# Feed-forward blocks: the first tile's attention scores in two groups of matmuls instead of one

## The chip, the cores and the metric

The kernel runs on one core of a Trainium2 chip. A core has five engines that work side by side: TensorE (matmuls, called PE in the profile, with PEld for the loading of its weights), VectorE (DVE), ScalarE (ACT), GpSimd (POOL) and SyncE (SP, which only issues transfers here). The metric is the device time of one execution in microseconds (us), lower is better.

A matmul on TensorE has a stationary operand, which is loaded into the array first (a weight load), and a moving operand, which streams past it. In the profile `64*128` ahead of a shape means that the stationary operand takes 64 rows and 128 columns of the array; `64x128` after it is the output or operand shape of one record. For 32-bit floats the profile shows each matmul of the program as two records of a matmul and two of a weight load.

## The reference, cut to what matters

The input is 16 sequences of 256 tokens with 128 features. Four blocks follow one another, each added to its input: a state-space block, a feed-forward block, a power-attention block, and the same feed-forward block again. The change touches the feed-forward blocks. Such a block has two layers, and each layer begins with local attention over 8 heads of 64 features, in windows of 64 tokens:

```python
bt = jnp.arange(n).reshape(w, WINDOW)            # WINDOW = 64, n = 256
sim = jnp.einsum('bhwid,bhwjd->bhwij', bq, bk)   # own window and the one before
mask = (i < j) | (i > j + WINDOW) | (j == -1)
sim = jnp.where(mask, -jnp.finfo(sim.dtype).max, sim)
attn = jax.nn.softmax(sim, axis=-1)
out = jnp.einsum('bhwij,bhwjd->bhwid', attn, bv)
```

A query sees the keys of its own window that are not later than itself, and those of the window before that are at most 64 tokens back. After the attention come a projection, a layer norm, a gated unit with 341 hidden features, and the residual sums.

## The kernel before, in words

**Tiles and stages.** In a feed-forward block (`ffn_block`, line 644) one item of work is one sequence in one layer, 32 items per block. An item's 256 tokens are two tiles of 128, called t = 0 and t = 1. Two items form a group, which later shares the gated unit. For each item and tile the stages of the attention are: project to queries, keys and values (`f_qk`, `f_pv`), rotate and normalise on VectorE and GpSimd (`f_m`), transpose on TensorE (`f_qkT_ps`, copied to `f_qkT`), lay the mask into a PSUM tile (`mask`, line 833, tile `f_sim`), add the scores to it (`scores`, line 840), take the row maximum (`maxima`, line 857, tile `f_mx`), subtract it, take the exponential and normalise (`f_pr`), transpose the weights (`f_ppt`, copied to `f_prT`), weigh the values (`weigh`, line 889, tile `f_po`) and project back (`f_pw`).

**The scores.** `f_sim` has 128 queries on the partitions and, along the free axis, two halves of heads (r), four head pairs (p) and 128 keys. Its two halves r lie in two PSUM banks. The mask copy puts 0 where a score counts and -1e30 where not; the matmuls accumulate on top of it. Head r of pair p lies in rows 64 r to 64 r + 63 of `f_qkT`, so that its matmul uses that half of the array's rows. For t = 0 all 128 queries meet all 128 keys in one matmul per head, eight in all: stationary 64 rows by 128 columns (the queries), moving 128 keys. For t = 1 each window of 64 queries meets the 128 keys of its window and the one before: sixteen matmuls, stationary 64 by 64, moving 128 keys. `weigh` is the reverse: for t = 0 eight matmuls with a stationary operand of 128 rows by 64 columns and 128 moving columns, for t = 1 sixteen with 128 by 64 and 64 moving columns.

**What sets the order.** Each engine runs its instructions in the order in which the program writes them: the class `Pinned` (line 69) ties every instruction to the one before it on its engine, and so line 89 is the line of nearly every record. Within the block the order is written by hand in the string `period` (line 1005): `s0.1:3` stands for `scores` of tile 0 of the second item of the group that was begun three periods earlier. One period holds two items' worth of every stage, so four calls of `scores`, two of them with t = 0. There are 16 periods of groups in a block, and a few more at the ends in which the pipeline fills and empties.

Of the kernel before, what the change touches and what calls it, by code (L numbers as in the profile page):

```python
# [20 lines left out]
P = 128  # L21
# [8 lines left out]
DH = 64  # L30
WINDOW = 64
# [15 lines left out]
def kernel(ctx: ExitStack, tc: tile.TileContext, io, out: bass.AP, blocks=BLOCKS):  # L47
# [515 lines left out]
    NP = HEADS // 2  # L563
# [80 lines left out]
    def ffn_block(k, fw, store):  # L644
# [14 lines left out]
        pe, dve, act, pool, sp = (Pinned(e) for e in (nc.tensor, nc.vector, nc.scalar, nc.gpsimd, nc.sync))  # L659
# [32 lines left out]
        psim = ps_sim.tile([P, 2, NP, P], F32, name=f"f{k}_sim_first", tag="sim")  # L692
# [146 lines left out]

        def scores(n, q, t):  # L840
            psim, qkT = q["sim", t], q["qkT"]
            for p in range(NP):
                for w in range(t + 1):
                    for r in range(2):
                        rows = slice(r * DH, (r + 1) * DH)
                        if t == 0:
                            out_, q0, nq, k0 = slice(0, P), 0, P, 0
                        else:
                            out_, q0, nq, k0 = (
                                slice(w * WINDOW, (w + 1) * WINDOW), P + w * WINDOW, WINDOW, (w + 1) * WINDOW  # L850
                            )
                        pe.matmul(
                            psim[out_, r, p, :], qkT[rows, 0, p, q0 : q0 + nq], qkT[rows, 1, p, k0 : k0 + P],
                            start=False, stop=True, skip_group_check=True,
                        )

        def maxima(n, q, t):
            mx = q["mx", t] = sb.tile([P, 2, NP], F32, name=f"f{k}_mx_{n}_{t}", tag="mx", bufs=4)
# [127 lines left out]
        def unit_sum(g, q):  # L986
# [10 lines left out]
            ns=norm_stats, nf=norm_factors, n=norm, ut=turn_tokens, uc=turned_tokens, p=project, sq=squares,  # L997
            ro=rotate, ss=square_sums, ra=rotated, v=values, vc=values_out, b=bounded, i=inverses,
            nw=newton, no=normed, t=turn, tc=turned, k=mask, s=scores, mx=maxima, lm=less_maximum,
            e=exponentials, su=sums, wo=weights_of, wt=turn_weights, wc=turned_weights, we=weigh,  # L1000
            oc=weighed, mi=mix, ma=mixed, Us=unit_stats, Uf=unit_factors, Un=unit_norm, Ut=unit_turn,
# [413 lines left out]
```

## Time and profile before

| | us |
|---|---|
| median of three runs | 2185.27 (2184.02 to 2185.98) |
| the profiled execution | 2186.17 |
| its span, from the first to the last instruction | 2184.2 |
| TensorE busy in the span | 2032.0 (93%) |
| GpSimd busy | 1900.1 (87%) |
| VectorE busy | 1839.4 (84%) |
| ScalarE busy | 1708.2 (78%) |

The first feed-forward block's score matmuls lie between 519 and 1115 us of the span, the second's between 1544 and 2140 us. The profile gives for each group of like instructions the shape, the count, the busy time, the mean of one and the idle time ahead of it. Its chain of waits follows back from the last instruction to what released each step; a stretch in which that chain holds one engine alone, piece after piece, is a stretch in which that engine sets the time.

### The profile page before, as it was taken

Reading aid. Unit: us, or ns where it says so; the run is one execution under the profiler, and the core shown is the slowest. Engines: PE = TensorE matmul, PEld = TensorE weight load, DVE = VectorE, ACT = ScalarE, POOL = GpSimd, SP = SyncE. Lnnn points to the kernel's source line nnn. Section 1 sums busy time; section 2 is a strip of 40 time slices with the busy share of each in tenths; the row PEclk is TensorE's granted clock in tenths of the full one; section 3 lists DMA queues with packets and bytes.
Section 4 is the critical chain, followed back from the end, with each engine's and each line's share of the span. In section 5 each row is a group of like instructions: output and inputs, shape, how many; then the busy total and the mean of one; then the engine's idle time right before and its main releaser. Section 6 shows DMA issues by size and latency. Waiting matters only on the chain.

```text
span 2184.2 us, 44223 instructions
## 1 busy us (share of the span) xinstructions
PE 2032.0 (93%) x16172; PEld 1333.4 (61%) x16174; DVE 1839.4 (84%) x3285; ACT 1708.2 (78%) x2879; POOL 1900.1 (87%) x2183
## 2 busy tenths in 40 slices
PE   5999999877999999999986999997899999999998
PEld 2344444334667777777773777775567777777775
DVE  1999999997988888888844999996999888888883
ACT  4777777746888887878854999997788887878874
POOL 6899999968999888888954999996999988888993
PEclk8999999998999999999996999999999999999999
DMA  4333333320100111101102332330010110001110
GB/s 91 97 83 81 98 80 78 80 49 20 24 23 16 23 23 23 23 16 23 23 11 82 118 118 86 112 118 2 21 24 22 23 23 17 23 22 33 28 28 23
DMA packets 97349, 104.21 MB, mean 48 GB/s; under 512 B 51458, under 2 KB 63596, under 8 KB 97132
## 3 DMA queue, kind: packets, MB, share of 16 engines
q1 hardware_dynamic: 96444, 101.22, 18.0%
q8 instruction: 129, 2.11, 0.4%
q14 instruction: 88, 0.72, 0.1%
q10 hardware_dynamic: 688, 0.15, 0.0%
HBM read 40.28 MB, written 2.36 MB: 20 GB/s over the span
## 4 chain that ended last, share of the span: by engine, by line
PE 58%; POOL 18%; DVE 11%; issue 8%; ACT 3%; DMA 1%; SPq 1%; POOLq 0%; DVEq 0%; ACTq 0%
PE f_qk L89 8%; POOL bx L89 7%; PE f_sim L89 5%; PE f_po L89 5%; PE f_pw L89 5%; PE f_qkT_ps L89 4%; PE f_ppt L89 4%; PE f_pv L89 4%; PE f1m_ag L89 3%; PE f3m_ag L89 3%; POOL f_m L89 3%; PE psc L89 3%; DVE z L89 2%; DVE hs L89 2%; DVE psc L89 2%
## 5 line engine op out<-in xcount | busy, mean ns | idle before, releaser
L89 POOL TENSOR_TENSOR f_m<-f_m 128x256 f32<-128x256 f32 x512 | 360.8, 729 | 30.9 <-DVE f_m L89 30.7
L89 DVE TENSOR_TENSOR f_m<-f_qk,rope 128x1024 f32<-128x1024 f32 x256 | 309.0, 1217 | 24.5 <-POOL f_m L89 16.4
L89 DVE TENSOR_TENSOR_SCAN hs<-a,bx 128x1024 f32<-128x1024 f32 x128 | 291.6, 2284 | 39.8 <-POOL bx L89 28.4
L89 POOL TENSOR_TENSOR bx<-dx,bb 128x1024 f32<-128x1024 f32 x128 | 298.7, 2361 | 4.6 <-DVE hs L89 3.9
L89 PE MATMUL f_qk<-wqkv,f_hT 128*128 128x512 f32 x512 | 261.8, 604 | 1.8 <-ACT f_hT L89 1.8
L89 POOL TENSOR_TENSOR f_m<-f_m,f_rn 128x512 f32<-128x512 f32 x256 | 263.3, 1045 | 0.2
L89 POOL TENSOR_TENSOR f_pr<-f_pr,f_rl 128x1024 f32<-128x1024 f32 x128 | 241.7, 1899 | 23.1 <-PE f_po L89 14.4
L89 PE MATMUL y_ps<-hs,ident 128*128 128x512 f32 x512 | 242.9, 599 | 11.5 <-DVE hs L89 6.6
L89 ACT ACTIVATE a<-delta,neg_a 128x510 f32<-128x510 f32 x256 | 176.1, 689 | 78.9 <-DVE hs L89 73.3
L89 ACT ACTIVATE f_sq<-f_qk 128x512 f32<-128x512 f32 x256 | 154.6, 605 | 60.5 <-PE f_qk L89 56.5
L89 ACT COPY f_qkT<-f_qkT_ps 128x512 f32<-128x512 f32 x256 | 147.3, 590 | 63.4 <-PE f_qkT_ps L89 62.7
L89 PEld LDWEIGHTS y_ps<-hs,ident 128*128 128x128 f32 x512 | 95.5, 190 | 154.6 <-issue 126.0
L89 POOL TENSOR_TENSOR z<-z,mx 128x1024 f32<-128x1024 f32 x96 | 180.8, 1896 | 7.9 <-DVE mx L89 5.6
L89 DVE TENSOR_REDUCE f_mx<-f_sim 128x8 f32<-128x1024 f32 x128 | 153.3, 1198 | 31.7 <-PE f_sim L89 31.7
L89 DVE TENSOR_REDUCE f_ss<-f_sq 128x8 f32<-128x512 f32 x256 | 173.0, 677 | 7.8 <-ACT f_sq L89 7.5
L89 PEld LDWEIGHTS f_qkT_ps<-ident,f_m 128*128 128x128 f32 x1024 | 121.2, 142 | 83.7 <-issue 50.9
L89 DVE TENSOR_TENSOR f_pr<-f_sim,f_mx 128x1024 f32<-128x1024 f32 x128 | 155.7, 1216 | 0.4
L89 PE MATMUL f_qkT_ps<-ident,f_m 128*128 128x128 f32 x1024 | 147.2, 277 | 9.4 <-POOL f_m L89 9.4
L89 DVE TENSOR_REDUCE f_rl<-f_pr 128x8 f32<-128x1024 f32 x128 | 152.9, 1194 | 1.9 <-ACT f_pr L89 1.9
L89 ACT COPY f_prT<-f_ppt 128x512 f32<-128x512 f32 x256 | 144.4, 595 | 6.5 <-PE f_ppt L89 5.8
L89 PE MATMUL f_sim<-f_qkT 64*64 64x128 f32 (+1 forms) x3072 | 145.6, 279 | 3.6 <-ACT f_sim L89 2.3
L89 PE MATMUL f_po<-f_prT,f_vx 128*64 128x64 f32 (+1 forms) x3072 | 144.4, 243 | 4.7 <-DVE f_m L89 2.4
(206 smaller groups left out, 5086.7 us busy)
## 6 DMA issues: line engine op xcount, KB each, us to landing
bb<-reps SPq DMA_DIRECT2D x128, 256.0 KB
pdk<-pngd SPq DMA_DIRECT2D x64, 512.0 KB
f_vx<-f_vx SPq DMA_DIRECT2D x128, 128.0 KB
f_shifted<-u_all SPq DMA_DIRECT2D x64, 64.0 KB
f_shifted<-u_all SPq DMA_DIRECT2D x64, 63.5 KB
x_all<-in_resid_dram SPq DMA_DIRECT2D x8, 256.0 KB
out_dram<-x_all SPq DMA_DIRECT2D x8, 256.0 KB
wqkv<-in_wqkv_dram SPq DMA_DIRECT2D x6, 256.0 KB
```

Source lines behind the costliest of these rows:

```text
L89: bi = getattr(self.eng, name)(*args, **kw)
```

## The change

Only `scores` changes, and only for t = 0. The eight matmuls become sixteen in two groups. The first group has all 128 queries as the stationary operand, as before, but only the first 64 keys as the moving one. The second group has the last 64 queries as the stationary operand (64 rows by 64 columns, output partitions 64 to 127) and the other 64 keys as the moving one. The quarter in which the first 64 queries meet the later 64 keys is wholly masked; it now keeps what the mask copy put there. For t = 1 the matmuls and their order are as before.

```diff
         def scores(n, q, t):
             psim, qkT = q["sim", t], q["qkT"]
-            for p in range(NP):
-                for w in range(t + 1):
-                    for r in range(2):
-                        rows = slice(r * DH, (r + 1) * DH)
-                        if t == 0:
-                            out_, q0, nq, k0 = slice(0, P), 0, P, 0
-                        else:
-                            out_, q0, nq, k0 = (
-                                slice(w * WINDOW, (w + 1) * WINDOW), P + w * WINDOW, WINDOW, (w + 1) * WINDOW
+            if t == 0:
+                pieces = [(slice(0, P), 0, 0, WINDOW, 0), (slice(WINDOW, P), WINDOW, WINDOW, WINDOW, WINDOW)]
+            else:
+                pieces = [
+                    (slice(w * WINDOW, (w + 1) * WINDOW), P + w * WINDOW, (w + 1) * WINDOW, P, 0) for w in range(2)
+                ]
+            for group in ([[c] for c in pieces] if t == 0 else [pieces]):
+                for p in range(NP):
+                    for out_, q0, k0, nk, at in group:
+                        for r in range(2):
+                            rows = slice(r * DH, (r + 1) * DH)
+                            nq = out_.stop - out_.start
+                            pe.matmul(
+                                psim[out_, r, p, at : at + nk], qkT[rows, 0, p, q0 : q0 + nq],
+                                qkT[rows, 1, p, k0 : k0 + nk], start=False, stop=True, skip_group_check=True,
                             )
-                        pe.matmul(
-                            psim[out_, r, p, :], qkT[rows, 0, p, q0 : q0 + nq], qkT[rows, 1, p, k0 : k0 + P],
-                            start=False, stop=True, skip_group_check=True,
-                        )
```

The order of everything else, on every engine, stays what it was, and so do the waits.

## The prediction

> **What bounds the kernel now.** I read the profile's summary page first, then a table of windows over the feed-forward blocks, then the chain of waits there, then the groups by shape. The summary says that TensorE is busy 93% of the span and holds 58% of the chain; both are averages. The windows show where it is full (columns: window in us; busy us and count for PE, PEld, DVE, ACT, POOL; granted clock, DMA share, GB/s):
>
> ```profile
> 640.00:700.00 60.00, 60.00 (x562) 42.81 (x559) 54.39 (x91) 52.48 (x93) 57.57 (x80) 1.00 0.09 21
> 700.00:800.00 100.00, 100.00 (x906) 71.66 (x905) 85.31 (x120) 81.06 (x141) 88.46 (x123) 1.00 0.09 21
> ...
> 1100.00:1180.00 80.00, 58.60 (x412) 40.42 (x410) 28.65 (x64) 36.66 (x60) 34.91 (x47) 0.81 0.15 40
> ```
>
> In the middle of a block TensorE is never idle, at full clock, while VectorE (85 of 100 us) and GpSimd (88) have slack. "Busy" alone is weak for matmuls, since they are pipelined and their ends are modelled. The chain of waits decides (start, length, what, count of records):
>
> ```profile
> 1073.28 0.86 PE f1m_ag L89 x2
> 1074.14 0.89 PE f_pw L89 x8
> 1075.03 1.09 PE f_sim L89 x16
> 1076.12 1.09 PE f_pw L89 x8
> ...
> 1082.40 0.87 PE f_ppt L89 x8
> 1083.27 1.02 PE f_po L89 x16
> 1084.29 1.03 PE f_sim L89 x32
> 1085.33 1.06 PE f_qk L89 x2
> 1086.38 0.86 PE f1m_ag L89 x2
> 1087.24 0.87 PE f_qkT_ps L89 x8
> 1088.12 1.08 PE f_po L89 x32
> 1089.20 1.09 PE f_pw L89 x8
> ```
>
> It is TensorE group after TensorE group, no wait on another engine between. That holds from 615.24 to about 1115 us in the first block and from 1640.51 to about 2140 us in the second; between 640 and 1110 us no matmul shape has any idle time before it (0.0 in each row). So TensorE time added there is added to the end one for one. Before 615.24 and 1640.51, while the pipeline fills, the chain runs through GpSimd and VectorE (`POOL f_m`, `DVE f_m`), and TensorE waits up to 1.2 us at a time.
>
> **Prices, from those lines.** `f_sim x16` is one call of the scores for t = 0: 16 records, 1.09 us. They run two at a time, one in each half of the array's rows, so 8 waves. `f_pw x8` takes 0.89 us after `f1m_ag` and 1.09 us after `f_sim`: 0.20 us for changing how the array is divided (draining it, then a first weight load of 128 columns with nothing to hide it). `f_qk x2` says the same: 0.86 against 1.06. So `f_sim x16` is 0.20 + 8 waves of 0.111.
>
> For a stationary operand of 64 columns the entry is cheaper by the shorter first load. By shape:
>
> ```profile
> L89 PEld LDWEIGHTS f_sim<-f_qkT 64*128 64x128 f32 x1024 | 62.7, 189 | 14.7 <-issue 4.5 <-ACT f_qkT L89 3.7 <-ACT f_sim L89 2.3
> L89 PEld LDWEIGHTS f_sim<-f_qkT 64*64 64x64 f32 x2048 | 55.2, 132 | 13.9 <-issue 7.8 <-ACT f_sim L89 2.3 <-ACT f_vx L89 1.5
> ```
>
> The mean load record is 189 ns with 128 columns, 132 ns with 64, the rows being the same 64. The difference, 0.057, is the half of a load that runs at some 0.11 us per 128 columns plus a fixed part. So entry is about 0.15 us for 64 columns (`f_qkT_ps x4` after `f_po`, 0.58 against 0.44 elsewhere, fits). From `f_po`: x16 is 8 waves with 64 stationary and 128 moving columns, (1.02 - 0.15) / 8 = 0.109 us; x32 is 16 waves with 64 and 64, (1.08 - 0.15) / 16 = 0.058 us. A wave therefore seems to last as long as the longer of its weight load and its stream, 0.11 us per 128 columns either way, the next load running under the present stream.
>
> **The change part by part.**
>
> *First group (A), 128 queries by 64 keys.* The stream falls from 0.107 to about 0.053 us a wave; the loads are the same 16 records of 128 columns. No row of the trace has a load longer than its stream, so I bound a wave: from below 0.058 us, the `f_po x32` wave (loads free); from above 0.165 us, load 0.11 and stream 0.055 one after the other. I take 0.111: the load alone already needs that, and in `f_sim` and `f_pw`, where both are 128 columns, the two together fit into 0.111, so they overlap. Only the last wave, with no load behind it, ends about 0.05 us sooner. A: 0.20 + 8 x 0.111 - 0.05 = 1.04 us.
>
> *Here a rule of the Trainium skill is weighed.* The page "TensorE: Matmul & The Clock Gate", section "Back-to-back issue gap", lets the gap between matmuls fall with the number of moving columns; by that alone A would be 0.20 + 8 x 0.058 = 0.66 us. Its section "LDWEIGHTS (loading the stationary operand)" says that a load takes columns / 1.2 ns whatever the rows: 107 ns for 128, 53 for 64, which is this trace's 57 ns of difference. This speaks against the change, since A halves the stream and leaves the load. The sum would be 0.38 us per call lower by the first rule; I go with the second, since the load rows carry it.
>
> *Second group (B), 64 queries by 64 keys.* All new: 8 matmuls, 16 matmul and 16 load records of 64 by 64, again two at a time. Price by `f_po x32`, which has 64-column loads and 64-column streams at the same rate of records: 8 x 0.058 = 0.46 us.
>
> *Between A and B.* The array goes from 64 x 128 to 64 x 64 divisions. The trace has no such step, but every step in which the columns change shows the price (`f_po` 128*64 to `f_pw` 128*128: 1.09 against 0.89). Bounds: nothing, B's first loads pulled under A, or 0.15 us. I take 0.15, as the change of columns alone is priced so elsewhere. "TensorEngine Tiling (Array Packing)", section "Key Properties", has it that a change of tiling mode, not of tile, drains the array; without the rule the sum would be 0.15 less. B: 0.61 us.
>
> *One call:* 1.04 + 0.61 - 1.09 = +0.56 us. After it the next group pays its entry of 0.20, as now.
>
> *Everything else.* The mask copy, the maximum and all later stages are the same instructions with the same waits; no DMA, no SP or POOL instruction moves. The maximum (`f_mx` on DVE) waits for B's last matmul and starts 0.56 us later relative to the group's start; behind it in VectorE's queue stand `f_ss` and `f_pr`, and ACT's exponential waits for those. Their slack (15 of 100 us on VectorE) takes that, since all of it moves with TensorE. The 1024 more matmul records and as many loads must be fetched; `f_po x32` already runs at B's rate of records with no idle time, so nothing is added.
>
> *How many count.* 64 calls: 1024 records of 64*128 / 16. In each block six start before 615.24 or 1640.51 and 26 after. 52 x 0.56 = 29.1 us on the path. Of the twelve early ones, one is on the chain, at a lower clock:
>
> ```profile
> 519.11 0.85 PE f_qkT_ps L89 x4
> 519.97 1.67 PE f_sim L89 x16
> 521.63 1.05 PE f_pv L89 x2
> ```
>
> It pays 0.56 x 1.67 / 1.09 = 0.86 us. The other eleven lie before TensorE waits for GpSimd or VectorE, which hide them; without that cover they would cost 6 us more. The sum is 29.1 + 0.9 = 30.0 us: span 2184.2 to 2214.2, the profiled execution's 2186.17 to 2216.2. The median of the runs shown is 0.9 us under that execution: **2215.3 us**, 1.4% slower. Anything within 0.2% (4.4 us) I count as the same, about what a measurement of this kernel can tell from no change.
>
> **Rivals.**
>
> 1. *Likeliest, 65%:* as above. Its own range is 2209 to 2222: a few hidden calls more or fewer, entry or wave off by a tenth, and the 6 us at the high end.
> 2. *No drain between A and B, 16%:* rows stay 64, and B's first loads go into the array under A's streams. For it: loads and streams overlap everywhere else. Against: each change of columns in the chain costs. 0.15 less per call: +0.41 x 52 + 0.6 = 22 us, 2207.
> 3. *The shorter stream pays, 10%:* A's waves at 0.058, by loads faster than their records say. 0.66 + 0.61 - 1.09 = +0.18, x 52 = 10 us with the early one, 2195. Against it the load rows.
> 4. *Load and stream don't overlap when the stream is short, 6%:* A's wave 0.165, +0.48 a call more, 1.04 x 52 = 54 plus 1, 2240. For it: no row shows a long load under a short stream.
> 5. *Not slower, 3%:* TensorE's fullness is an artefact of modelled ends, and another engine sets the period of about 39 us. Then the 1.13 us of two calls per period go into idle time, and it stays at 2185 to 2186. It decides once TensorE has 1.13 us of true slack per period (2.9%). For it: GpSimd at 88 of 100. Against: entries and groups have the same length each time and the chain has no other engine in it for 500 us.
>
> **How the numbers follow.** Cases 1 and 2 hold 81%; together they span 2202 to 2226 with 2207's and 2215's own errors, so that is the range; cases 3, 4 and 5 are out. Slower by over 0.2%: 1 to 4, 96% after 1% for a case 3 that shrinks into the noise; same 3%; faster 1%, for what I have not thought of.
>
> **What would show it.** In the profile after, the chain in mid-block should show the scores of t = 0 as 32 records in about 1.65 us. A at 0.9 us of starts for 8 waves confirms the load as the limit, 0.5 us refutes it. A gap of about 0.15 us from A's end to B's first wave confirms the drain, a B that follows at wave distance refutes it. B should need 0.46 us. The stretch from 615 to 1115 us should be 26 x 0.56 = 15 us longer, TensorE still full, and the state-space and power blocks unchanged. The prediction is wrong if that stretch grows by less than 10 or more than 20 us, or if VectorE or GpSimd enters the chain there.

## The result, and the profile after

| us | before | after |
|---|---|---|
| median | 2184.64 (2183.97 to 2185.98) | 2212.43 (2211.27 to 2213.36) |
| profiled execution | 2186.17 | 2213.05 |
| its span | 2184.2 | 2211.1 |
| TensorE busy | 2032.0 (93%) | 2064.9 (93%) |

The medians are those of four executions each. The kernel became slower: the ratio is 1.0122, with a 95% interval of 1.011 to 1.0134, that is 24 to 29 us of the 2184.64. The forecast was 2215.3 in a range of 2202 to 2226.

The chain of waits in the middle of the first feed-forward block, after the change (start, length, what, count of records):

```profile
1087.17 0.89 PE f_pw L89 x8
1088.06 1.65 PE f_sim L89 x32
1089.71 1.09 PE f_pw L89 x8
...
1096.86 1.02 PE f_po L89 x16
1097.88 1.03 PE f_sim L89 x32
1098.91 1.06 PE f_qk L89 x2
```

The 32 records of 1.65 us are the scores of tile 0, which were 16 records of 1.09 us. The other 32 records (1.03 us) are those of tile 1, unchanged; so are the other groups, to 0.01 us. No other engine has entered the chain there. The windows say the same: TensorE is full, and the others have a little more slack than before:

```profile
640.00:700.00 60.00, 60.00 (x573) 42.58 (x572) 52.73 (x89) 51.29 (x90) 55.69 (x79) 1.00 0.09 21
700.00:800.00 100.00, 100.00 (x981) 73.51 (x980) 82.73 (x116) 77.66 (x136) 86.34 (x119) 1.00 0.09 21
```

The matmul groups by shape (busy us, mean ns of one record) name the cause. First the scores of tile 0 before the change:

```profile
L89 PE MATMUL f_sim<-f_qkT 64*128 64x128 f32 x1024 | 74.9, 286 | 2.9 <-ACT f_sim L89 1.6 <-ACT f_qkT L89 1.3
```

And all scores after it:

```profile
L89 PE MATMUL f_sim<-f_qkT 64*128 64x64 f32 x1024 | 71.0, 278 | 1.9 <-ACT f_qkT L89 1.0 <-ACT f_sim L89 0.6
L89 PE MATMUL f_sim<-f_qkT 64*64 64x128 f32 x2048 | 70.7, 275 | 1.2 <-ACT f_sim L89 1.2
...
L89 PE MATMUL f_sim<-f_qkT 64*64 64x64 f32 x1024 | 43.6, 224 | 0.0
```

The first and the third row after the change stream the same 64 columns. The first, with a stationary operand of 128 columns, takes 278 ns a record, about as long as the second row, which streams 128; the third, with 64 stationary columns, takes 224. So a record of the first group lasts 54 ns longer for its weights. And those loads have not become cheaper or fewer:

```profile
L89 PEld LDWEIGHTS f_sim<-f_qkT 64*64 64x64 f32 x3072 | 90.0, 133 | 18.9 <-issue 7.5 <-ACT f_sim L89 2.8 <-ACT f_vx L89 1.5
...
L89 PEld LDWEIGHTS f_sim<-f_qkT 64*128 64x128 f32 x1024 | 62.1, 187 | 12.8 <-issue 4.2 <-ACT f_qkT L89 2.8 <-ACT f_sim L89 1.8
```

1024 loads of 128 columns, as before, and 1024 more of 64.

The start times of the single records show it without the modelled ends. In the call at 1066 us, after its first wave (a wave is the pair of records that run at a time), the waves of the first group start 0.112 us apart, and its loads of 128 columns too; from the third wave on those of the second group start 0.058 us apart. Between the last wave of the first group and the first of the second lie 0.209 us in place of 0.112, and the next wave follows after 0.106 us in place of 0.058: together 0.145 us more, at the one place where the array is divided anew.

**Where the time went.** From the `f_po` with which TensorE takes the chain over to the block's last `f_po`, the first block took 512.11 us before and 526.53 after, the second 511.95 and 526.45: +14.4 and +14.5, or 0.56 for each of 26 calls. Together that is 28.9 us. The whole span grew by 26.9; the other 2.0 come back elsewhere, almost all (1.9) between the blocks, where no code differs. The last three runs are about that.

### The profile page after: what moved, and what is told of

Read it like the earlier page. It is cut to its first block, busy times and chain, and to the rows that moved or that the text cites. A ratio compares the mean times of both kernels' runs of the same rounds, so it can differ in the third digit from the quotient of the medians.

```text
span 2211.1 us, 46271 instructions
## 1 busy us (share of the span) xinstructions
PE 2064.9 (93%) x17196; PEld 1367.4 (62%) x17198; DVE 1839.3 (83%) x3285; ACT 1705.9 (77%) x2879; POOL 1899.0 (86%) x2183
## 4 chain that ended last, share of the span: by engine, by line
PE 58%; POOL 17%; DVE 12%; issue 7%; ACT 4%; DMA 1%; SPq 0%; POOLq 0%; DVEq 0%; ACTq 0%
PE f_qk L89 8%; POOL bx L89 7%; PE f_sim L89 7%; PE f_po L89 5%; PE f_pw L89 5%; PE f_qkT_ps L89 4%; PE f_ppt L89 4%; PE f_pv L89 4%; PE f3m_ag L89 3%; POOL f_m L89 3%; PE f1m_ag L89 3%; DVE hs L89 3%; PE psc L89 3%; DVE z L89 2%; DVE psc L89 2%
## 5 line engine op out<-in xcount | busy, mean ns | idle before, releaser
L89 POOL TENSOR_TENSOR f_m<-f_m 128x256 f32<-128x256 f32 x512 | 360.1, 728 | 39.0 <-DVE f_m L89 37.1
L89 PE MATMUL f_sim<-f_qkT 64*64 64x128 f32 (+2 forms) x4096 | 180.7, 263 | 3.0 <-ACT f_sim L89 1.8
L89 PEld LDWEIGHTS f_sim<-f_qkT 64*64 64x64 f32 (+1 forms) x4096 | 152.1, 147 | 31.7 <-issue 11.6
```

The costliest lines, as they stand in the source:

```text
L89: bi = getattr(self.eng, name)(*args, **kw)
```

## The experiments

Beside the first four kernels the kernel before had a median of 2184.74 us (37 executions), beside the fifth 2183.71 (17); the last three runs are the kernel before itself. The theory is the prediction's: a wave of two matmuls lasts as long as the longer of its stream and its weight load, a change in how the array is divided costs a drain and an unhidden load, and TensorE is the path. The rivals are a stream that pays by itself, a price by the number of records, and a drain that does not exist.

### The first group alone

```diff
-pieces = [(slice(0, P), 0, 0, WINDOW, 0), (slice(WINDOW, P), WINDOW, WINDOW, WINDOW, WINDOW)]
+pieces = [(slice(0, P), 0, 0, WINDOW, 0)]
```

> The first group alone: all queries by the first 64 keys, the second group left out (so the last 64 queries miss the scores of the other 64 keys). If a wave lasts as long as its weight load of 128 columns, halving the stream gains only the end of the last wave: a call takes 0.20 + 8 x 0.111 - 0.05 = 1.04 us against 1.09 before, 52 calls on the path give -2.6 us, about 2182. If the stream sets the wave, a call takes 0.20 + 8 x 0.058 = 0.66 us and the whole falls by 22 us, to about 2162.

Measured: 2180.77 us, ratio 0.9981 (0.9975 to 0.9988), -4 us. The call in its chain of waits:

```profile
1050.62 1.04 PE f_sim L89 x16
1051.66 1.05 PE f_pv L89 x2
```

1.04 us, to the hundredth what the load rule gives; the two saturated stretches became 1.4 and 1.3 us shorter. Halving the streamed columns of all eight matmuls, and leaving out the rest of the work, gains 0.05 us of 1.09. That the shorter stream pays is refuted, and so is a load that waits for the stream to end, by which the call would have taken 1.52 us (0.20 + 8 x 0.165). The difference between this call and that of the change, 1.65 - 1.04 = 0.61 us, is the price of the second group.

### Two groups, the array divided alike

```diff
-... (slice(WINDOW, P), WINDOW, WINDOW, WINDOW, WINDOW)]
+... (slice(0, P), 0, WINDOW, WINDOW, WINDOW)]
```

> Two groups again, but the second one has all 128 queries as its stationary operand too, so that nothing changes in how the array is divided: as many streamed columns as before, twice the loads of 128 columns, no drain inside. If loads set the wave: 0.20 + 16 x 0.111 - 0.05 = 1.93 us a call, +0.84 x 52 = +44 us, about 2229, slower than the change itself by 16 us. If streamed columns set it: 0.20 + 16 x 0.058 = 1.13 us, +2 us. If the drain was what made the change slow: less than the change, under 2212.

Measured: 2227.6 us, ratio 1.0199 (1.0186 to 1.0212). The chain:

```profile
1050.56 0.89 PE f_pw L89 x8
1051.45 1.93 PE f_sim L89 x32
1053.38 1.09 PE f_pw L89 x8
```

This kernel streams exactly the columns of the kernel before, in the same division of the array, with no drain inside; only the weights are loaded twice. It pays 0.84 us a call for that, as forecast, and is slower than the change, which has the drain but loads half as many columns in its second group. Eight more waves of 128-column loads cost more here (1.93 - 1.04 = 0.89 us) than the new division and eight waves of 64-column loads together (0.61).

### Both windows in one group, 64 by 64

```diff
-pieces = [(slice(0, P), 0, 0, WINDOW, 0), (slice(WINDOW, P), WINDOW, WINDOW, WINDOW, WINDOW)]
+pieces = [(slice(0, WINDOW), 0, 0, WINDOW, 0), (slice(WINDOW, P), WINDOW, 0, P, 0)]
-for group in ([[c] for c in pieces] if t == 0 else [pieces]):
+for group in [pieces]:
```

> Both windows of queries in one group, as tile 1 has it: 64 queries by 64 keys and 64 queries by 128 keys, all with a stationary operand of 64 by 64. The same 32 records and the same skipped quarter as the change, without its second division and without loads of 128 columns. If loads, streams and drains are the whole price: 0.15 + 8 x 0.109 = 1.03 us a call against 1.09, -0.06 x 52 = -3 us, about 2181.5, faster than both kernels. If the doubled number of records is what costs: about 1.65 us a call, +28 us, 2212.

Measured: 2179.36 us, ratio 0.9977 (0.9969 to 0.9984), faster than both kernels. The chain, in which eight of the shorter records do not appear:

```profile
1052.25 0.44 PE f_qkT_ps L89 x4
1052.69 1.03 PE f_sim L89 x24
1053.72 1.06 PE f_pv L89 x2
```

The same 32 records as the change's, the same quarter left out, and 1.03 us in place of 1.65. So it is not the number of records that costs, but what the change loads and how often it divides the array anew. With 64 by 64 pieces four matmuls run at a time, one in each quarter of the array (the first four records of a call start within 0.02 us). The pieces with 64 keys do not wait for those with 128: in the call at 1052.6 us they start 0.058 us apart and the last of them starts at 0.46 us, while the long ones start 0.109 us apart to the end. The call lasts as long as eight streams of 128 columns. So the skipped quarter itself gains nothing: tile 1's calls skip no quarter and take 1.03 us too. By the prices of the working, what is gained against 1.09 is nearly all the cheaper entry with 64 columns, 0.15 in place of 0.20 us.

The stretches in which TensorE holds the chain are 1.6 and 1.4 us shorter than before, 2.9 in all, or 0.056 for each of 52 calls. The ratio says somewhat more, 3.5 to 6.8 us. In the two profiles the rest lies mostly in the tails of the blocks, where half the clock was granted for 3.4 us each here and for 10.2 and 6.8 us before; the section on the kernel before, below, is about that.

### The two groups mixed, pair by pair

```diff
-for group in ([[c] for c in pieces] if t == 0 else [pieces]):
+for group in [pieces]:
```

> The change's matmuls in another order: for each head pair the first group's two and then the second group's two, so that the division of the array changes eight times in a call and not twice. If each such change costs a drain and an unhidden first load: 4 x (0.20 + 2 x 0.111 - 0.05 + 0.15 + 2 x 0.058) = 2.55 us a call, +1.46 x 52 + 1 = +77 us, about 2262. If a step from 64 x 128 to 64 x 64 and back drains nothing: about 1.5 us a call, +21 us, 2206.

Measured: 2266.57 us, ratio 1.0375 (1.0357 to 1.0393). The chain:

```profile
1050.59 0.44 PE f_qkT_ps L89 x4
1051.02 2.52 PE f_sim L89 x32
```

The change's own matmuls, in another order, take 2.52 us in place of 1.65. Six more changes of division cost 0.87 us, 0.145 each on average: nearly the 0.15 that the prediction's working gives for both kinds (0.20 into the first group less 0.05 for its short last stream, 0.15 into the second). The saturated stretches grew by 37.1 us each, about 26 x 1.43. What a change of division is made of, a drain or a load that nothing hides, no run separates.

The kernel is 5 us slower than forecast, though, and the heads of the blocks are where more was lost than the forecast had. From the first scores to the `f_po` that stood at 615 us before, the first block took 105.1 us, against 95.4, and TensorE is on the chain there:

```profile
518.01 4.11 PE f_sim L89 x32
...
537.35 4.18 PE f_sim L89 x32
```

Both calls lie in stretches in which half the clock was granted, longer ones than before. The windows, first of the kernel before and then of this one (the granted clock is the number after POOL's):

```profile
517.80:521.00 3.20, 3.20 (x16) 1.99 (x16) 2.94 (x7) 2.37 (x4) 3.20 (x6) 0.50 0.00 0
531.50:534.70 3.20, 2.75 (x7) 1.17 (x5) 3.17 (x5) 3.18 (x6) 2.79 (x8) 0.50 0.02 5
```
```profile
516.10:526.10 10.00, 10.00 (x46) 6.28 (x45) 7.58 (x11) 3.96 (x9) 8.11 (x14) 0.50 0.02 6
536.60:546.60 10.00, 9.25 (x44) 6.17 (x45) 8.76 (x14) 3.31 (x8) 9.75 (x12) 0.50 0.06 13
```

Within this head half the clock was granted for 18.6 us, against 4.7 before. In the second block the head was given the half clock for 3.4 us in both kernels; there the six longer calls add 8.6 us, and the head took 97.9 us against 96.0, so that all but 1.9 was hidden. By that measure some 2 of the 9.7 us lost in the first head are cover that ran out, and the rest goes with the clock. Why the half clock lasted longer there, no run shows.

### The change for the first six calls of a block alone

```diff
-if t == 0:
+if t == 0 and n >= 6:
+    pieces = [(slice(0, P), 0, 0, P, 0)]
+elif t == 0:
```

> The change for the first six calls of each block alone, those that lie before TensorE takes the chain over; the other 26 calls of a block are as before. If TensorE's waits for GpSimd and VectorE hide all but one of the twelve: +0.5 to +0.9 us, about 2185.3. If nothing hides them: 12 x 0.56 = +6.7 us, about 2191.4.

Measured: 2185.14 us against 2183.71, ratio 1.0005 (0.9996 to 1.0013): no difference that can be told from nothing, and the upper end is 2.8 us, so that 6.7 is refuted. The chain at the place where TensorE takes over:

```profile
615.05 1.24 DVE f_m L89
616.29 0.04 issue
616.33 1.09 PE f_po L89 x16
```

VectorE still releases that `f_po`. TensorE's wait for it was 1.2 us in the profile of before and is 0.84 here. Over the whole head TensorE's idle time fell from 8.5 to 6.2 us, which is 2.3 of the 3.4 us by which the six calls grew; the head itself took 95.8 us against 95.4, within what the repeats of the kernel before show (95.1 to 95.9).

### The kernel before, three times more

> The kernel before once more, for one stretch of its profile: from the last group of f_po of the first feed-forward block to the first f_sim of the second it took 417.2 us in the profile of before and 415.3 us in that of the change, whose code there is the same. If that stretch varies from execution to execution, this profile gives another value within 2 us of those, and the 1.9 us say nothing about the change. If it is the change that shortens it, this profile gives 417.2 us again within 0.2.

> The kernel before a third time. In both of its profiles so far the last twelve matmul records of f1m_ag in the first block took 6.6 us from the first start to the last (several of them 0.85 us apart, twice the usual 0.43), against 4.83 us in all the changed kernels, and this is where the stretch between the blocks was 1.9 us longer. If the kernel's own timing fixes the clock granted there: 6.6 us again and a stretch of 417.2. If it is chance: at least one of the two repeats shows 4.8 us and a stretch of about 415.3.

> As the third: fixed by the kernel, 6.6 us for the last twelve records of f1m_ag in the first block and 417.2 us between the blocks; by chance, some other value between 4.8 and 8 us, and a stretch that follows it.

The three executions took 2186.1, 2185.9 and 2185.7 us. The stretch between the blocks came out at 417.2, 417.1 and 417.7 us. By the first expectation that would mean that the change shortens it. But the stretch has two parts, and they moved apart. The last twelve records of `f1m_ag` took 6.6 us from the first start to the last in the first two repeats and 4.8 in the third, which is the same kernel. The timeline of TensorE there, before (first profile), before (the last repeat) and after:

```profile
1145.63 7.17 PE L89 MATMUL f1m_ag<-f1m_hnT,w 128*128 128x512 f32 x12 [0.93 <-ACT f1m_hnT L89]
```
```profile
1143.77 5.42 PE L89 MATMUL f1m_ag<-f1m_hnT,w 128*128 128x512 f32 x12 [0.93 <-ACT f1m_hnT L89]
```
```profile
1160.04 5.42 PE L89 MATMUL f1m_ag<-f1m_hnT,w 128*128 128x512 f32 x12 [0.93 <-ACT f1m_hnT L89]
```

So the clock granted in the tail is not fixed by the kernel. From the last record of `f_po` to the start of the power block it was 28.8 us in three of the four profiles of before, 26.1 in the fourth, and 26.8 in that of the change. The 2.0 us between the first profile of before and that of the change are this. In the last repeat the power block itself then took 3.2 us longer than in the other three. The half clock lasted longer there too; tail and power block, before (first profile) and before (the last repeat):

```profile
1139.00:1149.10 10.10, 8.96 (x28) 6.60 (x29) 0.84 (x2) 2.75 (x3) 5.76 (x6) 0.50 0.00 0
1159.50:1200.30 40.80, 23.17 (x101) 15.19 (x102) 18.37 (x70) 17.41 (x36) 24.11 (x34) 0.50 0.35 108
```
```profile
1138.50:1141.80 3.30, 3.30 (x17) 3.30 (x17) 0.00 (x0) 0.00 (x0) 2.79 (x4) 0.50 0.00 0
1155.60:1206.60 51.00, 33.27 (x160) 22.68 (x161) 26.31 (x100) 25.14 (x47) 31.84 (x46) 0.50 0.40 128
```

In the tail half the clock was granted for 10.2 us in the one and 3.4 in the other, in the power block for 41.0 and 51.2. That fits the 3.2 us, though no run tests it. So a shorter tail need not make the whole shorter: the span of this repeat is 2183.7 us against 2184.2. What is left open is whether the kernel makes the one or the other clock likelier.

## Why the prediction was right, point by point

- *TensorE alone sets the time in the blocks.* Right. The stretches grew by 14.4 and 14.5 us where 26 x 0.56 = 14.6 were forecast, and only TensorE stands in the chain of their middle.
- *First group, 0.111 us a wave, by its loads.* Right. Alone it took 1.04 us (forecast 1.04), and twice of it in the same division 1.93 (forecast 1.93). The formula of the page "TensorE: Matmul & The Clock Gate", section "Back-to-back issue gap", by which the gap falls with the moving columns, would have made the call 0.66. The working did not say that the section itself keeps this formula for a matmul by itself and says that at few columns it comes out too low, since it has no room for the weight load; the 1.04 us agree with that remark, and with the load as the longer part.
- *Second group, 0.46 us, and 0.15 for dividing the array anew.* Right: 1.65 - 1.04 = 0.61 us. In the start times the new division shows as 0.145 us and the waves of the second group as 0.058 each, 8 x 0.058 = 0.46. The price of a new division was also tested by repeating it: 0.145 each again. That the array drains there, as the working has it, is one reading of this price; the runs show the price alone.
- *Records cost nothing by their number.* Right: with pieces of 64 by 64, 32 records took 1.03 us.
- *Eleven of the twelve early calls hidden.* Right for the change: with those calls alone changed, the time moved by less than 2.8 us. The waits that hide them are longer than the working reads: after the first scores TensorE waits up to 2.1 us at a time (`f_qkT_ps` for `f_m`), not 1.2. And the cover has an end, which the prediction did not work out: at +1.43 us a call some 2 us of a head were no longer hidden.
- *The twelfth, 0.86 us on the chain.* Not shown. The head of the first block, from the first scores to the `f_po` at 615 us, took 95.9 us after, against 95.4 before; but the repeats of before gave 95.1, 95.3 and 95.9, so that a term of this size can't be read there. In the profile after, the chain runs past this call through GpSimd.
- *The total, +30.0.* The profiles gave +26.9 and the medians +27.8, inside the range and 2 to 3 us under. In the profiles the term missing from the sum is the granted clock in the tail of the first block, 1.9 us, which the prediction had taken as fixed from one profile. That it is no larger is luck: the 37 executions of the kernel before lie up to 5.9 us apart. For the medians no profile shows where their 2 us are.

## What to carry to other kernels

In these runs a wave of 32-bit matmuls on a busy TensorE cost the longer of its stationary and its moving columns: 0.112 us with 128 by 128 and with 128 by 64 (stationary by moving), 0.109 with 64 by 128, 0.058 with 64 by 64. Skipping a masked piece paid only as far as it shortened the longer of the two: halving the moving columns under 128 stationary ones gained 0.05 us of 1.09, and eight waves for the rest cost 0.46 more. Count each change in how the array is divided as a step of its own (0.15 to 0.20 us here) and keep a group in one division; with all pieces 64 by 64 the call took 1.03 us, the fastest of all, by its cheaper entry and not by the skip. Read the price of such a piece from a row that has the same stationary and the same moving size, and where there is none, from the load.

## What the runs showed of the hardware that I had not expected

The clock granted to TensorE in the tail of a block, after it has idled for 4.5 us, differs between executions of one kernel and is worth 2 to 3 us of the tail. In the first profile of before the half clock reaches into the twelve records above, in that of the change it ends before them. The records are 0.85 us apart at first in the one and 0.43 in the other. In the kernel with the first six calls changed, the same happened in the second block's tail instead (7.9 us for the twelve, 4.8 in the first block).

The clock changes in steps. In all ten traces every stretch of half or full clock between two changes lasts a whole number of times 3.41 us, and the steps stand at a different place against the kernel's start in every execution. Where a step falls goes with what it costs: in the twenty tails, a half clock that begins 8.1 to 10.04 us after the last `f_po` record lasts 6.8 us (twelve tails), one at 10.05 us 13.7 (one), at 10.67 to 10.75 us 10.2 (three), and from 10.88 us on, when TensorE has just started again, 3.4 (four). Why it goes so, no run shows. The executions agree with it: of the 37 of the kernel before that were taken beside the first four experiments, the three with a mean granted clock of 0.975 took 2186.6 us on average, the two with 0.980 2183.6.

The Trainium skill, page "TensorE: Matmul & The Clock Gate", section "What's actually happening", describes such a clock of two steps, released by activity within a free-running window of 3413 ns; the 0.50 and 1.00 of these profiles agree with the two steps, and the 3.41 us and the shifting place of the steps with the window.
